# A softplus in a state-space kernel: the last sum moved to TensorE, two absolute values and relus to an eviction, and one product a chunk from GpSimd to VectorE

## The chip, the cores and the metric

The kernel runs on one core of one Trainium2 chip. A core has five engines with a queue each, worked off in order: TensorE (PE, with its weight loads PEld), VectorE (DVE), ScalarE (ACT), GpSimd (POOL) and SyncE (SP, which here only issues DMAs). The metric is device time in microseconds; the median of several runs is compared.

## What is computed

Two layers over one image of 64 x 64 positions (L = 4096) with 96 channels. Layer 0 is a two-dimensional selective scan and isn't touched. Layer 1 is a Mamba block with 192 inner channels and 16 states. Cut to what matters here:

```python
delta = jax.nn.softplus(jnp.einsum('blr,dr->bld', dt, W_dt) + b_dt)
dA = jnp.exp(delta[..., None] * A)
dBu = delta[..., None] * Bm[:, :, None, :] * xc[..., None]
def step(h, inp):
    dA_t, dBu_t, C_t = inp
    h = dA_t * h + dBu_t
    y = jnp.einsum('bdn,bn->bd', h, C_t)
    return (h, y)
```

`delta` is called dt in the kernel, `xc` is u, and delta times xc is w. The kernel computes softplus(x) as max(x, 0) plus S(|x|), where S is a product of two factors made from sigmoids and squares of |x|: acc, the first sigmoid, times (a square of q, plus SOFT_D).

## The kernel before

**Units.** Layer 1 is cut into four chunks of 1024 positions (CH). The 192 channels times 16 states of a chunk are done in 24 units of 128 rows, so 96 units s in all; a unit has step i = s mod 24 within its chunk. Three units in a row share the same two states: their B and C rows are the same, and they hold 64 channels each, once for either state. For each unit: dA = exp(A dt) on ScalarE (`decay`), f = B times w, the scan h over 1024 positions on VectorE (`scan`), h times C on GpSimd (`times_c`), and a sum over states into y on TensorE (`fold`, three units later).

**Who makes f.** The first unit of each group of three (s divisible by 3, `on_pool`) gets its f from GpSimd: B is loaded by DMA onto 128 rows (`load`), multiplied by w in place (`pool_f`, two units ahead), and dA is put into the PSUM tile f0. For the other two, TensorE spreads B over the rows into the PSUM tile f1 (`spread`), and VectorE multiplies it by w, into f0 or back into f1. So a VectorE instruction of the steady state has one operand in PSUM.

**Order.** The order on each engine is written out by hand: the class `Ordered` (L384, with the issuing call in L400, which is why nearly all instructions bear that line) chains each engine's instructions in the order of the calls in `run` (L2040). In each step s it calls: the next piece of `between` (L1944: the next chunk's projections, the last parts of its softplus, the former chunk's output), fillers on TensorE (`hold`), `spread` if s is divisible by 3, the loads, the decays of units s+1 or s+2, the next piece of `soft` (L2011), the unit's f and scan, then whatever `between` left as `late` on ScalarE, then `times_c` of unit s-1 and `pool_f` of unit s+2 on GpSimd, then the fold of unit s-3. `hold` (L1654) adds matmuls with zeros into an open y: they do nothing but keep TensorE busy.

**The next chunk's front.** While chunk c is scanned, chunk c+1 is prepared. `front_v` (L1518) makes dt's argument in three parts of 512 columns in the one PSUM bank `misc`, and ScalarE copies each to SBUF. `soft` then runs through the steps i, counted from at = 3 in chunk 0 and from 0 elsewhere: Abs of the whole dt to q at at+7; the two sigmoids (`soft_logistic`, L225) at at+9, for which ScalarE loads a table and then loads that of Exp again; the first Square at at+11. B of the next chunk, fetched as `flat`, is split into three bfloat16 parts by four small GpSimd instructions at at+10 (`split_b`, L1481: cast, subtract, cast, subtract), stored at at+13 and loaded at at+18; TensorE needs those parts for `spread`. `soft_parts` (L1987) does the rest in three steps (i = 16 to 18 in chunk 0, 13 to 15 in chunks 1 and 2): the second Square from q into PSUM on ScalarE (sq), then on VectorE `soft_times` (L245: (sq + SOFT_D) times acc) and max(dt, 0) plus that. At at+16 and at+17 GpSimd makes w = dt times u (`front_w`); dt and w are then copied by DMA onto the rows of the units (`front_dup`).

The last chunk has no next one, so `soft` and `soft_parts` do nothing in it.

Of the kernel before, what the change touches and what calls it, by code (L numbers as in the profile page):

```python
# [13 lines left out]
AF = mybir.ActivationFunctionType  # L14
ALU = mybir.AluOpType
# [10 lines left out]
P = 128  # L26
HALF = DI - P
GRP = 3
NB = 512
NCH = L // NB  # L30
CH = 1024
NSC = L // CH
# [5 lines left out]
UNIT = len(UNITS[0]) + len(UNITS[1])  # L38

PAIRS, GROUPS = NS // 2, DI // HALF  # L40
LAG = 3
WIDE = P
DUPS = {15: ((0, "dt"),), 16: ((1, "dt"),), 17: ((0, "w"),), 18: ((1, "w"), (2, "dt")), 19: ((2, "w"),)}

# [15 lines left out]
SOFT_ROOT = SOFT_K**0.5  # L60
# [164 lines left out]
def soft_logistic(nc, k, e, last, q):  # L225

    for to, i in ((last, 0), (q, 1)):
        nc.scalar.activation(to, e, AF.Sigmoid, scale=-1.0, bias=k["soft"][:, i : i + 1])


def soft_square(nc, k, q, i):

    nc.scalar.activation(
        q, q, AF.Square, scale=(1.0, SOFT_ROOT)[i], bias=k["soft"][:, 2 + i : 3 + i]
    )
# [9 lines left out]
def soft_times(nc, last, q, out):  # L245

    nc.vector.scalar_tensor_tensor(out, q, SOFT_D, last, ALU.add, ALU.mult)
# [1058 lines left out]
class Layer1:  # L1306
# [171 lines left out]
            flat, self.bc_dram[0, c].rearrange("n (j k) -> (n j) k", k=NS * CH // P)  # L1478
        )

    def split_b(self, c):  # L1481

        nc, b = self.nc, self.chunks[c]["flat"]
        self.at = c
        self.chunks[c]["split"] = parts = self.tile("flat", [P, 3, NS * CH // P], "split", BF16)
        nc.gpsimd.tensor_copy(parts[:, 0, :], b)
        nc.gpsimd.tensor_sub(b, b, parts[:, 0, :])
        nc.gpsimd.tensor_copy(parts[:, 1, :], b)
        nc.gpsimd.tensor_sub(parts[:, 2, :], b, parts[:, 1, :])

    def store_b(self, c, queue=None):
        (queue or self.nc.sync).dma_start(
# [25 lines left out]
    def front_v(self, c, q):  # L1518
        nc, of = self.nc, self.chunks[c]
        if "dt" not in of:  # L1520
            self.at = c
            of["dt"] = self.tile("dt", [P, CW], "dt")
            of["acc"], of["q"] = self.tile("sp", [P, CW], "acc"), self.tile("sp", [P, CW], "q")
        ps = self.misc(c, [P, NB], f"pv{q}")
        yield from self.steps(
            self.product(ps, q, self.dt_taps(of["dbl"])),
            lambda: nc.scalar.copy(of["dt"][:, self.part(q)], ps),
        )

    def front_w(self, c, col, engine):  # L1530
        of = self.chunks[c]
# [28 lines left out]
        return self.chunks[c]["dup"][i % GROUPS][name]  # L1560

    def on_pool(self, s):
        return s % GROUPS == 0 and 0 < s < NSC * UNIT

    def load(self, part, s):

        if s >= NSC * UNIT:
            return
        name, (c, i) = "BC"[part], divmod(s, UNIT)
        self.at = s  # L1570
        self.units[s][name] = to = self.tile(name, [P, CH], name)
        for share, state in enumerate(UNITS[1][i // GROUPS]):
            row = self.bc_dram[part, c, state : state + 1, :]
            self.nc.sync.dma_start(to[self.half1(share), :], row.to_broadcast([HALF, CH]))
# [25 lines left out]
    def scan(self, s):  # L1600
        self.at, of = s, self.units[s]
        c, i = divmod(s, UNIT)
        if not self.on_pool(s):
            if i % GROUPS == (1 if s > GROUPS else 0):
                self.f = self.tile("f", [P, CH], "f0")
            of["f"] = self.b if i % GROUPS == 2 else self.f
            self.nc.vector.tensor_mul(of["f"], self.b, self.of_unit("w", s))
        of["h"] = self.tile("h", [P, CH + SHIFT], "h")
        self.nc.vector.tensor_tensor_scan(
            of["h"][:, SHIFT:], of["dA"], of["f"], self.last[:, i : i + 1] if c else 0.0,  # L1610
            ALU.mult, ALU.add,
        )
# [41 lines left out]
    def hold(self, s, ahead):  # L1654

        c, i = divmod(s, UNIT)
        at = i - (3 if c == 0 else 0)
        if c == NSC - 1 and i:
            n = 0 if 7 <= i <= 12 else 1 if not ahead else 2 if i % GROUPS == 0 else 0
        else:  # L1660
            n = ({0: 1, 9: 1, 12: 1, 15: 1} if ahead else {-2: 2, -1: 1, 1: 2, 12: 1, 13: 2, 14: 2, 15: 2}).get(at, 0)
        open_y = [(k, g) for k, g in ((c, 2), (c, 0), (c - 1, 2)) if self.is_open(s - ahead, k, g)]
        for _ in range(n if open_y else 0):
            k, g = open_y[0]
            self.nc.tensor.matmul(
                self.chunks[k][f"y{g}"], self.k["zero"], free(self.k["within"], (1, NB)),
                start=False, stop=False,
            )
# [130 lines left out]
    def start(self):  # L1799
# [17 lines left out]
        dbl = of["dbl"] = self.tile("dbl", [ROWS, CH], "dbl")  # L1817
        acc, sq = of["acc"], of["q"] = [self.tile("sp", [P, CW], n) for n in ("acc", "q")]
        dt = of["dt"] = self.tile("dt", [P, CW], "dt")
# [32 lines left out]
            do(self.product(pv[p], p, self.dt_taps(dbl)))  # L1852
        self.flat_b(0)
        self.load(1, 0)
        self.split_b(0)
        self.store_b(0, nc.gpsimd)

        next_u = self.chunks[1]
# [128 lines left out]
    def soft_parts(self, c):  # L1987

        of = self.chunks[c]
        for p in range(3):  # L1990
            col = self.part(p)
            ps = self.misc(c, [P, NB], f"sq{p}")
            self.late = lambda: self.nc.scalar.activation(
                ps, of["q"][:, col], AF.Square, scale=SOFT_ROOT, bias=self.k["soft"][:, 3:4]
            )
            yield
            soft_times(self.nc, of["acc"][:, col], ps, ps)
            self.nc.vector.scalar_tensor_tensor(
                of["dt"][:, col], of["dt"][:, col], 0.0, ps, ALU.max, ALU.add
            )  # L2000

    def all_between(self):
        for c in range(NSC):
# [7 lines left out]
    def soft(self, c):  # L2011

        at = 3 if c == 0 else 0
        for i in range(UNIT):
            if c + 1 < NSC:
                nc, k = self.nc, self.k
                dt, acc, q = (self.chunks[c + 1].get(n) for n in ("dt", "acc", "q"))
                if i == at + 7:
                    nc.scalar.activation(q, dt, AF.Abs)
                elif i == at + 9:  # L2020
                    soft_logistic(nc, k, q, acc, q)
                elif i == at + 11:
                    soft_square(nc, k, q, 0)
                elif i == at + 6:
                    self.flat_b(c + 1)
                elif i == at + 10:
                    self.split_b(c + 1)
                elif i == at + 13:
                    self.store_b(c + 1)
                elif i == at + 18:  # L2030
                    self.load_b(c + 1)
                elif i == at + 16:
                    self.front_w(c + 1, slice(0, CH), nc.gpsimd)
                elif i == at + 17:
                    self.front_w(c + 1, slice(CH, CW), nc.gpsimd)
                for g, name in DUPS.get(i - at, ()):
                    self.front_dup(c + 1, g, names=(name,))
            yield

    def run(self):  # L2040
# [5 lines left out]
        for s in range(n):  # L2046
# [30 lines left out]
            if self.on_pool(s + 2):  # L2077
                self.pool_f(s + 2)
            if s >= LAG:
                if s < n - 1:  # L2080
# [191 lines left out]
```

## Time and profile before

| | us |
|---|---|
| median of 3 runs | 521.02 (519.98 to 521.06) |
| the profiled execution | 520.83 |
| its span in the profile | 519.0 |
| first scan of chunk 0, 1, 2, 3 (start) | 182.24, 262.38, 344.37, 427.70 |
| last scan ends | 507.6 |

| steady rows of layer 1 | count | mean ns |
|---|---|---|
| GpSimd h<-h,C, 128x1024 | 95 | 2395 |
| GpSimd B<-B,w, 128x1024 | 31 | 2373 |
| VectorE scan h<-dA,last,f, 128x1024 | 47 | 2347 |
| VectorE f<-f,w, 128x1024 | 65 | 1221 |
| ScalarE dA<-dt,A, 128x1024 | 65 | 1140 |
| ScalarE table load | 24 | 1283 |
| TensorE y<-within,zeros (the fillers), 128x512 | 134 | 652 |

A row of the profile names the line, engine, operation, output <- inputs by the program's tile names, their shapes, the count, and the time. In a timeline a row has the start and the duration, and in brackets how long the engine stood idle before it and what released it. Rows of one engine overlap by up to 0.1 us, so what a repeated instruction costs is read from one start to the next. Times are from the start of the span.

### The profile page before, as it was taken

What the parts mean: (1) busy time and instruction counts of PE and PEld (TensorE: products, weight loads), DVE (VectorE), ACT (ScalarE), POOL (GpSimd) and SP (SyncE); (2) the same over time, 40 slices, a digit from 0 to 9 for tenths busy, and PEclk for the clock granted to TensorE, in tenths of its full rate; (3) what the DMA queues carried; (4) which work ended last, traced back from release to release, by engine and by line L of the source; (5) the groups of instructions that cost most, each with busy time, mean ns of one, the idle gap of its engine ahead of it and who ended that gap; (6) DMA issues with size and microseconds to landing.
All of it is one profiled execution on the core that took longest, in us unless ns stands there. A gap on an engine that the chain in (4) does not pass through costs nothing. (4 is left out here: it accounts for less than half of the span.)

```text
span 519.0 us, 5048 instructions
## 1 busy us (share of the span) xinstructions
PE 454.0 (87%) x1487; PEld 171.6 (33%) x1487; DVE 450.5 (87%) x458; ACT 310.4 (60%) x475; POOL 368.3 (71%) x249
## 2 busy tenths in 40 slices
PE   4999999989879999887768988879689979987994
PEld 3445446546533323222112322212112322222323
DVE  6896999946661899989999999989999999999993
ACT  4637996378735896893395883475783366253220
POOL 8034010017620669999999999998999999999980
PEclk9997999999999999999799989979968989998898
DMA  6100930000000584435993446973536993454301
GB/s 180 30 5 12 257 129 0 0 1 1 2 31 5 144 206 126 132 82 133 234 215 97 124 126 153 232 186 80 132 82 140 235 237 82 122 136 97 81 0 38
DMA packets 28536, 55.90 MB, mean 108 GB/s; under 512 B 13186, under 2 KB 14974, under 8 KB 28244
## 3 DMA queue, kind: packets, MB, share of 16 engines
q1 hardware_dynamic: 26596, 53.58, 42.4%
q10 hardware_dynamic: 1808, 1.72, 1.1%
q8 instruction: 13, 0.21, 0.2%
q0 software_dynamic: 96, 0.20, 0.2%
q14 instruction: 23, 0.19, 0.1%
HBM read 41.86 MB, written 2.65 MB: 86 GB/s over the span
## 5 line engine op out<-in xcount | busy, mean ns | idle before, releaser
L400 POOL TENSOR_TENSOR h<-h,C 128x1024 f32<-128x1024 f32 x96 | 226.7, 2383 | 11.4 <-DVE h L400 6.8
L400 DVE TENSOR_TENSOR_SCAN h<-dA,last,f 128x1024 f32<-128x1024 f32 (+1 forms) x48 | 111.6, 2325 | 4.6
L400 PE MATMUL y<-h,both 128*64 128x512 f32 x382 | 113.4, 673 | 1.0 <-POOL h L400 1.0
L400 ACT ACTIVATE f<-dt,A 128x1024 f32<-128x1024 f32 x31 | 34.7, 1118 | 89.9 <-DVE h L400 89.8
L400 DVE TENSOR_TENSOR f<-f,w 128x1024 f32<-128x1024 f32 x65 | 79.3, 1221 | 4.7 <-PE f L400 2.4
L400 POOL TENSOR_TENSOR B<-B,w 128x1024 f32<-128x1024 f32 x31 | 73.5, 2373 | 2.0 <-DMA B<-bc_dram 2.0
L400 ACT ACTIVATE dA<-dt,A 128x1024 f32<-128x1024 f32 x65 | 73.6, 1140 | 1.7 <-DMA dt<-dt 1.7
L400 PE MATMUL y<-within,zeros 128*128 128x512 f32 x134 | 72.0, 652 | 0.0
L400 DVE TENSOR_TENSOR_SCAN h<-f,last,B 128x1024 f32<-128x1024 f32 x24 | 55.9, 2328 | 0.0
L400 PE MATMUL pc<-pad,cw 96*128 96x464 f32 (+1 forms) x144 | 54.9, 540 | 0.5 <-ACT v L400 0.5
L400 PEld LDWEIGHTS y<-h,both 128*64 128x64 f32 x382 | 23.3, 146 | 65.9 <-issue 43.6
L400 DVE TENSOR_TENSOR_SCAN h<-dA,f 128x1024 f32<-128x1024 f32 x17 | 38.9, 2287 | 1.5
L400 PEld LDWEIGHTS y<-within,zeros 128*128 128x128 f32 x134 | 23.0, 196 | 49.5 <-issue 49.5
L400 PE MATMUL f<-parts,pick 48*128 48x512 bf16 x62 | 20.7, 418 | 20.3 <-DVE h L400 20.3
L400 PEld LDWEIGHTS pc<-pad,cw 96*128 96x128 f32 x144 | 28.3, 199 | 27.0 <-issue 22.4
L400 ACT ACT_TABLE_LOAD x24 | 30.8, 1283 | 2.1 <-PEq L2262 1.7
L400 POOL TENSOR_SCALAR ln_small<-ln_small 128x4 f32<-128x4 f32 x8 | 1.9, 236 | 37.4 <-DVE ln_small L400 35.7
L400 POOL MEMSET wda<- 128x4 f32 (+3 forms) x8 | 1.0, 120 | 31.1 <-ACT wda L400 31.1
L400 PE MATMUL pc<-xn,cw 96*64 96x512 f32 (+1 forms) x60 | 21.5, 601 | 0.7 <-ACT xn L400 0.7
L400 PE MATMUL po<-v,w_o 128*128 128x256 f32 (+1 forms) x48 | 15.5, 458 | 3.0 <-DVE x L400 2.3
L400 PE MATMUL po<-sz,w_out 128*128 128x512 f32 x36 | 18.0, 610 | 0.0
L400 PEld LDWEIGHTS <-pick 48*128 48x128 bf16 x62 | 4.0, 96 | 41.1 <-DVE h L400 22.7
(236 smaller groups left out, 713.9 us busy)
## 6 DMA issues: line engine op xcount, KB each, us to landing
C<-bc_dram SPq DMA_DIRECT2D x64, 256.0 KB, 5.0
B<-bc_dram SPq DMA_DIRECT2D x62, 256.0 KB, 4.0
dt<-dt SPq DMA_DIRECT2D x12, 256.0 KB, 4.5
w<-q SPq DMA_DIRECT2D x12, 256.0 KB, 5.8
dt<-dt SPq DMA_DIRECT2D x18, 128.0 KB, 6.0
w<-q SPq DMA_DIRECT2D x18, 128.0 KB, 4.7
wB<-rows_dram SPq DMA_DIRECT2D x1, 1472.0 KB
wC<-rows_dram SPq DMA_DIRECT2D x1, 1472.0 KB
```

The source lines that it names most:

```text
L400: ins = it(*args, **kw)
```

## The change

- dt's eviction becomes two ScalarE instructions: relu into dt, absolute value into q. The single Abs at at+7 goes.
- The sigmoids come a step earlier (at+8); both Squares run over all 1536 columns from SBUF to SBUF (at+11, at+12).
- In each of the three steps of `soft_parts`, VectorE makes acc = (q + SOFT_D) times acc with all operands in SBUF; TensorE adds dt and acc in `misc` by two matmuls with the identity; ScalarE copies the sum to dt.
- `split_b` becomes two halves: cast on ScalarE and subtraction on GpSimd at at+9, the same again at at+11. In the start of the layer GpSimd still does all.
- Unit 18 of each chunk but the last (OFF_POOL) gets its f from VectorE: no B load and no GpSimd product, dA in SBUF, and unit 17's f goes to f0 so that f1 is free for the spread of unit 18.
- The fillers at at+13 to at+15 go: seven matmuls a chunk.

```diff
+OFF_POOL = 18
...
-    def split_b(self, c):
+    def split_first(self, c, cast=None):
 
         nc, b = self.nc, self.chunks[c]["flat"]
         self.at = c
         self.chunks[c]["split"] = parts = self.tile("flat", [P, 3, NS * CH // P], "split", BF16)
-        nc.gpsimd.tensor_copy(parts[:, 0, :], b)
+        (cast or nc.scalar.copy)(parts[:, 0, :], b)
         nc.gpsimd.tensor_sub(b, b, parts[:, 0, :])
-        nc.gpsimd.tensor_copy(parts[:, 1, :], b)
-        nc.gpsimd.tensor_sub(parts[:, 2, :], b, parts[:, 1, :])
+
+    def split_rest(self, c, cast=None):
+
+        b, parts = self.chunks[c]["flat"], self.chunks[c]["split"]
+        (cast or self.nc.scalar.copy)(parts[:, 1, :], b)
+        self.nc.gpsimd.tensor_sub(parts[:, 2, :], b, parts[:, 1, :])
...
-        ps = self.misc(c, [P, NB], f"pv{q}")
-        yield from self.steps(
-            self.product(ps, q, self.dt_taps(of["dbl"])),
-            lambda: nc.scalar.copy(of["dt"][:, self.part(q)], ps),
-        )
+        ps, col = self.misc(c, [P, NB], f"pv{q}"), self.part(q)
+
+        def evict():
+            nc.scalar.activation(of["dt"][:, col], ps, AF.Relu)
+            nc.scalar.activation(of["q"][:, col], ps, AF.Abs)
+
+        yield from self.steps(self.product(ps, q, self.dt_taps(of["dbl"])), evict)
...
     def on_pool(self, s):
-        return s % GROUPS == 0 and 0 < s < NSC * UNIT
+        c, i = divmod(s, UNIT)
+        return s % GROUPS == 0 and 0 < s < NSC * UNIT and (i != OFF_POOL or c == NSC - 1)
...
-        if s >= NSC * UNIT:
+        if s >= NSC * UNIT or part == 0 and not self.on_pool(s):
...
-            if i % GROUPS == (1 if s > GROUPS else 0):
+            if i % GROUPS == 0 or i % GROUPS == 1 and self.on_pool(s - 1):
                 self.f = self.tile("f", [P, CH], "f0")
-            of["f"] = self.b if i % GROUPS == 2 else self.f
+            of["f"] = self.b if i % GROUPS == 2 and self.on_pool(s + 1) else self.f
...
-            n = ({0: 1, 9: 1, 12: 1, 15: 1} if ahead else {-2: 2, -1: 1, 1: 2, 12: 1, 13: 2, 14: 2, 15: 2}).get(at, 0)
+            n = ({0: 1, 9: 1, 12: 1} if ahead else {-2: 2, -1: 1, 1: 2, 12: 1}).get(at, 0)
...
-            ps = self.misc(c, [P, NB], f"sq{p}")
-            self.late = lambda: self.nc.scalar.activation(
-                ps, of["q"][:, col], AF.Square, scale=SOFT_ROOT, bias=self.k["soft"][:, 3:4]
-            )
+            dt, acc = of["dt"][:, col], of["acc"][:, col]
+            soft_times(self.nc, acc, of["q"][:, col], acc)
+            ps = self.misc(c, [P, NB], f"sum{p}")
+            for i, term in enumerate((dt, acc)):
+                self.nc.tensor.matmul(ps, self.k["ident"], term, start=i == 0, stop=i == 1)
+            self.late = lambda: self.nc.scalar.copy(dt, ps)
             yield
-            soft_times(self.nc, of["acc"][:, col], ps, ps)
-            self.nc.vector.scalar_tensor_tensor(
-                of["dt"][:, col], of["dt"][:, col], 0.0, ps, ALU.max, ALU.add
-            )
...
-                if i == at + 7:
-                    nc.scalar.activation(q, dt, AF.Abs)
+                if i == at + 8:
+                    soft_logistic(nc, k, q, acc, q)
                 elif i == at + 9:
-                    soft_logistic(nc, k, q, acc, q)
+                    self.split_first(c + 1)
                 elif i == at + 11:
                     soft_square(nc, k, q, 0)
+                    self.split_rest(c + 1)
+                elif i == at + 12:
+                    soft_square(nc, k, q, 1)
                 elif i == at + 6:
                     self.flat_b(c + 1)
-                elif i == at + 10:
-                    self.split_b(c + 1)
```

More of the change, by code (lines that the diff above doesn't have):

```diff
@@ L1854, in start @@
         self.load(1, 0)
-        self.split_b(0)
+        self.split_first(0, nc.gpsimd.tensor_copy)
+        self.split_rest(0, nc.gpsimd.tensor_copy)
         self.store_b(0, nc.gpsimd)
@@ L2016, in soft @@
                 nc, k = self.nc, self.k
-                dt, acc, q = (self.chunks[c + 1].get(n) for n in ("dt", "acc", "q"))
-                if i == at + 7:
-                    nc.scalar.activation(q, dt, AF.Abs)
+                acc, q = (self.chunks[c + 1].get(n) for n in ("acc", "q"))
+                if i == at + 8:
+                    soft_logistic(nc, k, q, acc, q)
                 elif i == at + 9:
-                    soft_logistic(nc, k, q, acc, q)
+                    self.split_first(c + 1)
                 elif i == at + 11:
                     soft_square(nc, k, q, 0)
+                    self.split_rest(c + 1)
+                elif i == at + 12:
+                    soft_square(nc, k, q, 1)
                 elif i == at + 6:
                     self.flat_b(c + 1)
-                elif i == at + 10:
-                    self.split_b(c + 1)
                 elif i == at + 13:
```

## The prediction

> **What bounds the kernel now.** I read the busy shares first, then the VectorE timeline from 180 us on, then GpSimd's and ScalarE's beside it, and last the few places where VectorE and GpSimd both read SBUF.
>
> ```profile
> PE 454.0 (87%) x1487; PEld 171.6 (33%) x1487; DVE 450.5 (87%) x458; ACT 310.4 (60%) x475; POOL 368.3 (71%) x249
> ```
>
> The shares average two layers, so they don't decide. The VectorE timeline of chunk 0 does (start, duration; idle in brackets):
>
> ```profile
> 227.09 2.29 DVE L400 TENSOR_TENSOR_SCAN h<-dA,f 128x1024 f32<-128x1024 f32 x1
> 230.51 2.29 DVE L400 TENSOR_TENSOR_SCAN h<-f,B 128x1024 f32<-128x1024 f32 x1 [1.14 <-POOL B L400]
> ...
> 236.45 0.67 DVE L400 SCALAR_TENSOR_TENSOR sq<-sq,acc 128x512 f32<-128x512 f32 x1
> 237.16 0.69 DVE L400 SCALAR_TENSOR_TENSOR dt<-dt,sq 128x512 f32<-128x512 f32 x1
> 237.76 1.23 DVE L400 TENSOR_TENSOR f<-f,w 128x1024 f32<-128x1024 f32 x1
> ```
>
> From the first scan (182.24) to the last (507.6) VectorE stands still four times: 1.14 us here, 1.45 at 346.7, 0.43 and 0.49 in the last chunk. VectorE is the bound of layer 1; what is taken from it or put on it counts in full. GpSimd runs beside it almost without a gap:
>
> ```profile
> 219.48 4.73 POOL L400 TENSOR_TENSOR h<-h,C 128x1024 f32<-128x1024 f32 x2
> 224.17 0.28 POOL L400 CAST split<-flat 128x128 bf16<-128x128 f32 x1
> ...
> 225.78 2.40 POOL L400 TENSOR_TENSOR h<-h,C 128x1024 f32<-128x1024 f32 x1
> 228.11 2.37 POOL L400 TENSOR_TENSOR B<-B,w 128x1024 f32<-128x1024 f32 x1
> ```
>
> It starts a product every 2.335 us (7.0 for three), and its B<-B,w feeds a scan: ended at 230.48, scan of unit 15 started at 230.51. A group of three units costs VectorE 9.43 to 9.61 us and GpSimd 4 x 2.335 = 9.34. GpSimd has no slack for a long wait. ScalarE has idle time, but in bursts; this is the burst that matters:
>
> ```profile
> 216.47 1.12 ACT L400 ACTIVATE f<-dt,A 128x1024 f32<-128x1024 f32 x1
> 217.53 1.13 ACT L400 ACTIVATE dA<-dt,A 128x1024 f32<-128x1024 f32 x1
> ...
> 221.29 1.28 ACT L400 ACT_TABLE_LOAD   x1
> 222.59 1.58 ACT L400 ACTIVATE acc<-q,soft 128x1536 f32<-128x1536 f32 x1
> 224.19 1.58 ACT L400 ACTIVATE q<-q,soft 128x1536 f32<-128x1536 f32 x1
> ...
> 225.96 1.28 ACT L400 ACT_TABLE_LOAD   x1
> 227.26 1.12 ACT L400 ACTIVATE f<-dt,A 128x1024 f32<-128x1024 f32 x1
> ```
>
> **Part by part.** All of it happens three times, for chunks 1 to 3 while chunks 0 to 2 are scanned; the fourth chunk's steps stay.
>
> VectorE, removed: three pairs of 512 columns, each 236.45 to 237.76 = 1.31 us: -3.93 a chunk. Added: three single acc products, about 0.62 each by the same rows: +1.86. Added: unit 18's f. A unit with f on VectorE takes 3.57 us (two from 276.00 to 283.16), one with GpSimd's product 2.42 (283.16 to 285.59): +1.15. Sum -0.9 a chunk, -2.7 in all.
>
> GpSimd: a B product (2.335) and two casts (0.36 each) go, 3.1 a chunk. As VectorE is the bound this is worth at most the 1.14 us above. SP's queue loses two loads a chunk: nothing, since GpSimd waited for a B load only once (2.03 us before 189.07), and that load stays.
>
> ScalarE: Abs over 1536 (1.48) becomes three of 512 at eviction (nearest rows: a copy from PSUM 0.58, an Identity 0.69), three squares of 512 (0.68) become one of 1536 (1.56), three evictions (0.58) and two casts are new: 2 to 3 us more. From 200 to 290 us ScalarE is busy 59.73 of 90, so the amount costs nothing; its order does.
>
> **The hand-over of the split.** The first subtraction on GpSimd now waits for a cast on ScalarE, and behind it on GpSimd's queue stand the h products and the next B product that a scan needs. The order of the built program puts the cast behind: decay, decay, table load, two sigmoids, u's eviction, table load, decay. Chunk 0: the two decays end 218.58; table and sigmoids 4.39 (221.29 to 225.68) to 222.97; u 0.58, last 0.08, table 1.30, decay 1.05: 225.98. The cast on ScalarE has no row: between a 128x1 copy (0.18) and a 128x384 copy (0.46); I take GpSimd's own 0.28. Cast done 226.3. GpSimd is at that place at 221.8, where h of unit 10 ends. So it stands 4.5 us. Then 0.43 for the subtraction and 7.0 for h, h, B: 233.8. Unit 15's scan starts there and not at 230.51: +3.3, with the old 1.14 inside.
> Chunk 1, the same chain from 289.31 (decays to 291.40, +4.39, +0.58, +0.09, +1.30, +1.05, +0.28): cast 299.1, where GpSimd is free at 292.8; B product out at 306.6, and the scan of that chunk's unit 12 was at 302.37: +4.25. Chunk 2 from 372.65 has no u: cast 381.85, B at 389.35 for 385.71: +3.65. Sum +11.2. The decay behind the sigmoids is in time (298.8 for a scan at 300.1); the last Square too (ends near 306.4 without any wait, acc then comes after 308.8).
>
> **The acc product reads q and acc, both in SBUF**, where sq was in PSUM; in steady state no VectorE operation of this kernel has two SBUF inputs. The start of the layer has some, VectorE first:
>
> ```profile
> 172.28 0.69 DVE L400 SCALAR_TENSOR_TENSOR acc<-q,acc 128x512 f32<-128x512 f32 x1
> 178.33 1.09 DVE L400 SCALAR_TENSOR_TENSOR acc<-q,acc 128x512 f32<-128x512 f32 x1
> ```
> ```profile
> 177.85 1.04 POOL L400 COPY dt<-dt 64x512 f32<-64x512 f32 x1
> 178.83 1.07 POOL L400 COPY w<-q 64x512 f32<-64x512 f32 x1
> ```
>
> The second took 0.40 longer: it seems to begin when GpSimd's copy ends, and GpSimd's next copy took 1.07 where others take 0.62. The Trainium skill, "SBUF — State Buffer", section "Who interferes with whom", speaks against this edit: a VectorE instruction with two SBUF inputs and a GpSimd one that reads SBUF exclude each other, and the later waits until the earlier is over. By the uncontended row acc costs 0.62; by the rule, up to one whole product more (0 to 2.34 each, 0 to 21 us for nine). The copies are short, so the rows alone can't choose; I take the rule and work out the phase. Let the late B product end at 0: scan to 2.26; GpSimd does the second subtraction (0.43) and h to 2.77: acc waits 0.5. GpSimd goes on about 0.55 late: h to 5.65, h to 8.0; the next acc comes at 6.95 and waits 1.05; the third comes at 12.2 with h running until 13.3: 1.1. Together 2.6 a chunk, the same in each, because the same product starts the clock: +7.8.
>
> **TensorE.** Six matmuls against ident for seven fillers a chunk, both 128x512 (the fillers take 0.65, started every 0.43 to 0.5): nothing. In chunks 1 and 2 the third sum is in step 15, its spread is needed one scan later: hidden, with about 1 us to spare. In chunk 0 the third sum stands in step 18 directly ahead of spread(18), and unit 18's f, now on VectorE, needs that at once: after acc one matmul (0.5, by the fillers), the spread (0.60, the row at 241.37), two hand-overs of some 0.05: +1.2, once; bounds 0.6 (if spread overlaps) and 2 (if TensorE comes cold: the two fillers at 345.06 took 2.08). dt's copy out of PSUM comes later than the vector addition did, but w and the copies of dt wait on steps far behind: nothing, up to 1 if the covering group were gone.
>
> **Sum:** 11.2 + 7.8 - 2.7 + 1.2 = +17.5 us. The profiled execution took 520.83 (span 519.0, 1.8 around it), 0.2 under the median; so 521.0 + 17.5 = 538.5, and a span of 536.5.
>
> **Rivals.**
> GpSimd is not held, and the trade is worth its face. If the cast were there when GpSimd comes (before 221.8, 292.8 and 376.1, so 4.5 to 6.4 us earlier than worked out), GpSimd, 3.1 us lighter, would run ahead and wait for each scan; acc would start with the scan's end and be first. -2.7 - 1.1 + 1.2 gives 518.4. For it: GpSimd already waits 0.2 to 0.7 for scans in chunks 1 and 2. Against: the table load can't move ahead of the decays, which wait for scans. 7%.
> Held, but no exclusion: 521.0 + 9.7 = 530.7. For it: only short copies show the exclusion. 17%.
> Exclusion, but a hand-over mostly hidden: about 521.0 + 5 = 526. 7%.
> A harder exclusion, each acc waiting nearly a whole product, or GpSimd's next one going first: 8 to 13 us more, 547 to 552. 9%.
> As worked out, 534 to 543: 58%. 2% for no change.
>
> **How the numbers follow.** The likeliest case gives 538.5. The range reaches to the case without exclusion and to the upper side of the likeliest: 529 to 543. A measurement here tells 0.2% (1 us) from no change: faster 0.07, within 0.02, slower 0.91.
>
> **What would show it.** Right: in the profile after, GpSimd's small flat subtraction has 4 to 6.5 us idle before it, released by ScalarE; VectorE's scans of unit 15 (chunk 0) and 12 (chunks 1 and 2) wait 3.7 to 4.5 for B; acc<-q,acc lasts 1.2 to 1.8 instead of 0.69, and the h product after it 0.5 longer; in chunk 0 one f waits about 1.2 for TensorE. Wrong: acc at 0.69 takes off 7.8; no idle ahead of the subtraction takes off 11.2; a long wait for q or for dt would be something that I put at nothing.

## The result, and the profile after

| | before | after |
|---|---|---|
| median, us | 521.04 (519.98 to 522.67, 4 runs) | 553.35 (549.0 to 555.77, 4 runs) |
| ratio to before | | 1.0608, 95% interval 1.0534 to 1.0682 |
| profiled execution; its span | 520.83; 519.0 | 549.0; 547.1 |
| first scan of chunk 0, 1, 2, 3 to the first of the next chunk (chunk 3: to the start of its last scan) | 80.14, 81.99, 83.33, 78.63 | 86.91, 94.13, 92.65, 77.91 |

Slower by 32 us, where 17.5 was predicted. A ratio leaves out executions far above the fastest of their kernel (four of six in e1, four of 22 in e14), so it needn't be that of the two medians. The profiled execution is the fastest of the four after; the account below is of it, 28 us above the profiled one of before.

The busy shares of after, to be held against the first line of the prediction:

```profile
PE 456.4 (83%) x1481; PEld 171.9 (31%) x1481; DVE 464.0 (85%) x452; ACT 315.5 (58%) x490; POOL 362.1 (66%) x240
```

VectorE has six instructions less and is busy 13.5 us longer: some instruction of it has become slow. Every chunk with a next one is longer, by 6.8, 12.1 and 9.3 us; the last, which the change hardly touches, is not. The VectorE timeline of after in chunk 0 (start, duration, what, and in brackets the idle time ahead of it):

```profile
224.46 1.23 DVE L401 TENSOR_TENSOR f<-f,w 128x1024 f32<-128x1024 f32 x1 [0.90 <-PE f L401]
...
236.22 2.29 DVE L401 TENSOR_TENSOR_SCAN h<-f,B 128x1024 f32<-128x1024 f32 x1 [4.62 <-POOL B L401]
238.43 1.02 DVE L401 SCALAR_TENSOR_TENSOR acc<-q,acc 128x512 f32<-128x512 f32 x1
...
250.38 1.23 DVE L401 TENSOR_TENSOR f<-f,w 128x1024 f32<-128x1024 f32 x1 [1.75 <-PE f L401]
```

The scan waits 4.62 us for GpSimd's B, and unit 18's f 1.75 for TensorE: both were foretold (4.44 and 1.2). The wait of the f at 224.46 was not. GpSimd's timeline there:

```profile
228.79 0.43 POOL L401 TENSOR_TENSOR flat<-flat,split 128x128 f32<-128x128 f32 x1 [6.17 <-ACT split L401]
229.18 4.69 POOL L401 TENSOR_TENSOR h<-h,C 128x1024 f32<-128x1024 f32 x2
233.84 2.35 POOL L401 TENSOR_TENSOR B<-B,w 128x1024 f32<-128x1024 f32 x1
```

That is the hand-over as worked out: the subtraction stands 6.17 us for ScalarE's cast (7.2 and 6.0 in chunks 1 and 2), then come h, h and the B that the scan needs. What was not foretold is in chunk 1 (all engines; rows of several engines and PE's weight loads left out):

```profile
315.70 2.35 DVE L401 TENSOR_TENSOR_SCAN h<-f,last,B 128x1024 f32<-128x1024 f32 x1 [4.56 <-POOL B L401]
315.94 7.03 POOL L401 TENSOR_TENSOR h<-h,C 128x1024 f32<-128x1024 f32 x3
...
317.97 7.85 DVE L401 SCALAR_TENSOR_TENSOR acc<-q,acc 128x512 f32<-128x512 f32 x1
...
322.84 2.43 POOL L401 TENSOR_TENSOR B<-B,w 128x1024 f32<-128x1024 f32 x1
...
329.49 2.68 POOL L401 TENSOR_TENSOR h<-h,C 128x1024 f32<-128x1024 f32 x1 [4.22 <-DVE h L401]
```

One product of 512 columns, 0.67 us by itself, takes 7.85. It starts behind its scan at 317.97 and ends at 325.82, 0.55 after GpSimd's B product ended at 325.27: it lasted through the rest of one h product, two more, and the B product. GpSimd ran dry only because the scan that releases its next h stands behind this very product. Chunk 2 shows the same (7.88); in chunk 0 the three took 1.02, 1.75 and 0.67, and the first two of these got in when GpSimd's running product ended, although its next one was ready. The second and third of chunks 1 and 2 took 0.67, since GpSimd was waiting then.

How the stretch from the first scan to the start of chunk 3's last sums up, by the table of stretches (us, then busy time of each engine), before and after:

```profile
sum 324.09, PE 283.03 PEld 81.90 DVE 311.94 ACT 189.05 POOL 310.28; mean PE 70.76 PEld 20.48 DVE 77.98 ACT 47.26 POOL 77.57
```
```profile
sum 351.60, PE 285.38 PEld 82.09 DVE 325.94 ACT 194.05 POOL 304.09; mean PE 71.35 PEld 20.52 DVE 81.49 ACT 48.51 POOL 76.02
```

27.5 us longer: VectorE is busy 14.0 us more and idle 13.5 more. GpSimd's 6.2 less are worth nothing.

| term of the sum | predicted | in the profile after |
|---|---|---|
| hand-over: VectorE's waits for B | +11.2 | 4.62 + 4.56 + 3.79, less the old 1.14: +11.8 |
| acc's waits for GpSimd | +7.8 | nine acc, 21.8 us, less 9 x 0.67: +15.8 |
| the trade on VectorE | -2.7 | busy +14.0 less those 15.8: -1.8 |
| f waiting for TensorE | +1.2 | 0.90 + 1.75 + 0.60 + 0.35, less the old 1.45 + 0.43 + 0.49: +1.2 |
| sum | +17.5 | +27.0 |

The 0.5 us that the sum lacks are gaps too short to be listed.

### The profile page after: what moved, and what is told of

Its sections match the earlier page's. It is cut to its first block, busy times and chain, and to the rows that moved or that the text cites. A ratio compares the mean times of both kernels' runs of the same rounds, so it can differ in the third digit from the quotient of the medians.

```text
span 547.1 us, 5030 instructions
## 1 busy us (share of the span) xinstructions
PE 456.4 (83%) x1481; PEld 171.9 (31%) x1481; DVE 464.0 (85%) x452; ACT 315.5 (58%) x490; POOL 362.1 (66%) x240
## 5 line engine op out<-in xcount | busy, mean ns | idle before, releaser
L401 DVE TENSOR_TENSOR_SCAN h<-dA,last,f 128x1024 f32<-128x1024 f32 (+1 forms) x50 | 116.3, 2326 | 5.1
L401 DVE TENSOR_TENSOR f<-f,w 128x1024 f32<-128x1024 f32 x68 | 83.1, 1222 | 6.0 <-PE f L401 3.6
L401 ACT ACTIVATE dA<-dt,A 128x1024 f32<-128x1024 f32 x68 | 77.1, 1141 | 12.2 <-DVE h L401 11.2
L401 POOL TENSOR_TENSOR B<-B,w 128x1024 f32<-128x1024 f32 x28 | 66.4, 2372 | 1.5 <-DMA B<-bc_dram 1.5
L401 DVE TENSOR_TENSOR_SCAN h<-f,last,B 128x1024 f32<-128x1024 f32 x22 | 51.3, 2331 | 8.3 <-POOL B L401 8.3
L401 PE MATMUL y<-within,zeros 128*128 128x512 f32 x92 | 50.1, 652 | 0.0
L401 PE MATMUL sum<-acc,ident 128*128 128x512 f32 x18 | 11.7, 738 | 19.0 <-DVE acc L401 19.0
L401 ACT COPY dt<-sum 128x512 f32<-128x512 f32 x9 | 5.3, 586 | 36.2 <-PE sum L401 36.2
L401 PEld LDWEIGHTS y<-within,zeros 128*128 128x128 f32 x92 | 15.3, 194 | 33.3 <-issue 33.3
L401 DVE SCALAR_TENSOR_TENSOR acc<-q,acc 128x512 f32<-128x512 f32 x12 | 24.5, 2045 | 0.0
```

Source lines behind the costliest of these rows:

```text
L401: ins = it(*args, **kw)
```

## The experiments

Two theories at first. Mine: the hand-over's place costs its 11 us whatever else happens, and acc costs more than worked out because GpSimd instructions whose inputs are ready go first. The rival: acc is late for another reason (its Square, the order on VectorE), and the second SBUF operand is a bystander. "Port" stands below for whatever keeps a VectorE product with two SBUF operands and a GpSimd product from running at once. For reference, the kernel before took 520.98 beside e1 to e4, 522.13 beside e5 to e7, 521.58 beside e8 to e11, 520.96 beside e13 and e14, and 520.94 beside e18.

**e1, the changed kernel once more.**

> The changed kernel once more, unaltered, to see how much the long acc differs from one execution to the next. Queue theory (GpSimd keeps the read port for as long as its next instruction is ready, and whether acc gets in between two of them is decided by a few hundredths of a microsecond): the times spread over 549 to 556 us and the first acc of at least one chunk has another length than 1.02, 7.85 and 7.88. Data theory (acc waits for one GpSimd instruction at most, and the 7.85 comes from an operand that is late in chunks 1 and 2): the same lengths in the same chunks. Both: the idle time ahead of the flat subtraction is 6.2, 7.2 and 6.0 again.

555.11 (545.66 to 555.67), ratio 1.0524 (1.047 to 1.0578), where the medians alone give 1.066. The profiled execution is one of 555.54. The waits for B were 4.65, 4.56 and 3.82; acc took 7.87 and 7.95 in chunks 1 and 2, and in chunk 0, on the timeline:

```profile
236.38 7.05 POOL L401 TENSOR_TENSOR h<-h,C 128x1024 f32<-128x1024 f32 x3
238.29 5.69 DVE L401 SCALAR_TENSOR_TENSOR acc<-q,acc 128x512 f32<-128x512 f32 x1
```

The same place that took 1.02 us in the first profile takes 5.69 here, again until GpSimd's third h had ended. So this is an outcome that can fall either way. The nine acc took 25.5 us, not 21.8, and VectorE waited 5.9 us for f, not 3.6: together 6.0 of the 6.5 us between the two profiled executions. The idle time ahead of the flat subtraction, put at 6.2, 7.2 and 6.0 again by both theories, was 8.55 in chunk 1, with the same wait for B.

**e2, acc with one SBUF operand.** The second Square goes to PSUM, part by part, as before.

```diff
-            soft_times(self.nc, acc, of["q"][:, col], acc)
+            soft_times(self.nc, acc, of["sq"], acc)
```

> The changed kernel with the second Square put into PSUM in three parts as before, so that acc has one SBUF input; the sum on TensorE and the hand-over of the split stay. Queue theory: every acc takes 0.67, VectorE wins back the 15.8 us that they are over 0.62 each in the profile after (549.0), less about 0.5 because TensorE can't start a sum early: 533 to 535, with the waits of 4.6, 4.6 and 3.8 for B unchanged. Data theory: the first acc of chunks 1 and 2 stays long, over 545.

538.88 (535.67 to 539.91), ratio 1.0326 (1.0287 to 1.0365). The acc row:

```profile
L401 DVE SCALAR_TENSOR_TENSOR acc<-sq,acc 128x512 f32<-128x512 f32 x9 | 6.1, 675 | 0.9 <-ACT sq L401 0.9
```

All nine take 0.66 to 0.69. The waits for B stay (13.1 us). So the second SBUF operand holds some 14 us. The time missed the 533 to 535 expected: VectorE's waits for f grew from 3.6 to 7.2 us.

**e3, the casts back on GpSimd at at+10, all else as changed.**

> The changed kernel with the two casts back on GpSimd at at+10, so that GpSimd waits for nothing there; acc stays in SBUF. Hand-over theory: the waits of the scans for B (4.62, 4.56, 3.79) fall to at most 1.2 together, about 11.8 us less by themselves; GpSimd then has another phase when acc comes, so the accs can take from 0.67 to 8 each: 535 to 545 against 553. If the waits for B came from GpSimd's load and not from the cast, they stay and the time is 550 or more.

535.04 (534.25 to 536.38), ratio 1.0281 (1.0248 to 1.0314). No scan waits for B any more. The first acc of each chunk still stands (3.41, 1.68 and 6.40 us), and VectorE now comes earlier and waits for the Square as well:

```profile
DVE acc L401 <- ACT q L401: 3.7, 3, 1.7
```

**e4, both undone.**

> Both undone: acc reads its square from PSUM and GpSimd casts for itself; the relu and Abs at eviction, the sum on TensorE and unit 18's f on VectorE stay. If port and hand-over are the whole loss, what is left is the trade at face value: 3 x (-2.07 + 1.15) = -2.8 on VectorE, +1.8 to 2.3 for f of unit 18 in chunk 0 behind the third sum, up to -1.1 for the old wait for B: 519 to 521. If there is a third cause, over 523.

528.3 (525.29 to 530.37), ratio 1.0145 (1.011 to 1.018). This missed what I expected by 7 us: a third cost had been covered by the first two. VectorE's waits in it (total, times, longest):

```profile
DVE f L401 <- PE f L401: 8.0, 8, 2.6
DVE acc L401 <- ACT sq L401: 2.5, 3, 1.1
```

Before, the same stretch had none for a Square, and for f:

```profile
DVE f L400 <- PE f L400: 2.4, 3, 1.4
```

**e5, the hand-over at a better place.** e2, with ScalarE's casts at at+9 and at+12 and GpSimd's subtractions two steps behind them; the store moves to at+15 (diff against e2).

```diff
                 elif i == at + 11:
...
+                    self.minus_first(c + 1)
...
+                elif i == at + 14:
+                    self.minus_rest(c + 1)
```

> As the run with the Square in PSUM, with the split still shared by ScalarE and GpSimd, but GpSimd's two subtractions stand later in its queue (at+11 and at+14, store at at+15), where ScalarE's casts have long been done. The work is the same, only the place differs. Hand-over theory: no idle ahead of the subtractions, no wait of a scan for B over 0.5: 518 to 521. If the cost of the hand-over were that of the handing itself (a semaphore between two engines), 530 or more.

529.73 (528.73 to 531.3), ratio 1.0155 (1.0108 to 1.0202); no wait for B. That is e4's time, which has no hand-over at all: handing work over costs nothing measurable there; standing for it at the head of GpSimd's queue does. The 518 to 521 expected were missed by 9 us, as in e4 by the third cost (waits of 8.1 us for f and 4.7 for a Square).

**e6, the hand-over alone, in the kernel before** (with the sigmoids at at+8).

> The kernel before with the split's hand-over alone: sigmoids at at+8, casts on ScalarE, subtractions on GpSimd at at+9 and at+11; nothing else changed. Hand-over theory: scans wait about 4.6, 4.6 and 3.8 for B, 12 us less the old 1.1: 531 to 533. If the hold only comes about together with the other edits: 521 to 523.

533.59 (531.39 to 536.03), ratio 1.0205 (1.0151 to 1.0259): +11.5, against +11.2 worked out.

```profile
DVE h L400 <- POOL B L400: 12.9, 3, 4.6
```

**e7, the second SBUF operand alone, in the kernel before.** The second Square, one of 1536 columns at at+12, writes SBUF, and the nine products read it there.

```diff
-            soft_times(self.nc, of["acc"][:, col], ps, ps)
+            soft_times(self.nc, of["acc"][:, col], of["q"][:, col], ps)
```

> The kernel before with the port's edit alone: the second Square stays in SBUF over all 1536 columns, and the nine products with acc read both factors from SBUF and write to PSUM as before. One-instruction theory (the prediction's): each waits 0 to 2.3 us for GpSimd, so 9 x 1.2 = 10 at a middling phase and 21 at most: 525 to 542. Queue theory: single products wait for more than one GpSimd instruction, up to where GpSimd's next one needs a scan that stands behind the product: some last 3 to 10 us, the time is 530 to 560. No port at all: 521.

541.77 (541.54 to 541.93), ratio 1.0375 (1.033 to 1.042): +19.6. The nine products together:

```profile
L400 DVE SCALAR_TENSOR_TENSOR sq<-q,acc 128x512 f32<-128x512 f32 x9 | 25.2, 2796 | 0.0
```

At 0.67 each they would be 6.0; the other 19.2 are the loss. The first of each chunk took 6.13, 4.89 and 5.50, the second 0.67, the third 2.2. The total alone fits both theories (525 to 542 and 530 to 560); these lengths, over 0.67 + 2.34, fit only the one without the bound of one instruction. The operand alone, with nothing else of the change, does it: the rival falls.

**e8 to e11: the third cost.** Each is e4 with one thing set back: the seven fillers (e8), the sigmoids at at+9 (e9), unit 18's f on GpSimd (e10). e11 sets all three back; in it each acc comes a step behind its Square, and part of dt is copied onto the units' rows before its sum is in, so that some rows have the relu alone.

> The kernel with both causes undone (split's products in PSUM, casts on GpSimd), and the seven filler products at steps 13 to 15 of a chunk restored, nothing else. What is left open by that kernel's 528.3 us are some 5 us that neither cause holds, and its VectorE shows short waits for TensorE's f (0.35 and 0.54 a chunk, 1.60 and 0.66 beside the accumulation). If those come of a TensorE that has cooled without its fillers, the waits of 0.35 and 0.54 go and the time falls to 525 to 526. If they come of the places of the products and sigmoids, the fillers change nothing or cost something: 528 to 529.

> Both causes undone, and the sigmoids back at step 9 from step 8. The theory for the third cause: u's eviction stands behind the earlier sigmoids on ScalarE and so holds its PSUM bank, and the next products of TensorE and an f behind them are late (1.60 and 0.66 us in the profile of both undone). Then those two waits go, and the time is 525.5 to 527. Against it: if the sigmoids' place doesn't matter, 528 to 529; the Squares then come later too, and the accumulation may wait for them longer than the 0.80, 0.63 and 1.07 it waits now (up to 1 us more each), which would take the gain back.

> Both causes undone, and unit 18's second f back on GpSimd in every chunk, so that this part of the change is undone as well. By the sum of the prediction VectorE then has 1.15 us less in each of three chunks, and the wait of 2.61 us of that f for TensorE in chunk 0 is gone: 528.3 less 3.45 less 2.6 = 522.2. Against it: GpSimd gets 2.2 us more in each of those chunks, and if its order with the scans was already tight there (it had no slack of its own left in the later steps), the scans wait for B by up to as much and the time stays at 526 to 529.

> The part that gives, alone: relu and absolute value at dt's eviction and the sum on TensorE, with the Squares into PSUM and dt copied out by ScalarE at the end of its step; fillers, sigmoids at step 9, unit 18's f on GpSimd and the casts on GpSimd all as in the kernel before. If the trade on VectorE is worth what the prediction put on it (two operations on the scans' engine removed and one left in each of nine places, 2.07 us a chunk, three chunks), 521.0 less 6.2 = 514.8, and 515 to 518 with some waits of the accumulation for its Square. If GpSimd is the bound in these chunks once VectorE is shorter (it has about as much to do as VectorE), the time stays at 519 to 521. Over 523 would say that the sum on TensorE itself costs what it saves.

| kernel | median, us | ratio to before |
|---|---|---|
| e4 | 528.3 | 1.0145 (1.011 to 1.018) |
| e8 | 537.09 (534.39 to 540.76) | 1.0317 (1.0284 to 1.035) |
| e9 | 530.77 (528.72 to 536.61) | 1.0217 (1.0176 to 1.0258) |
| e10 | 521.23 (518.48 to 524.59) | 0.9998 (0.9976 to 1.002) |
| e11 | 530.33 (529.61 to 533.76) | 1.0201 (1.0169 to 1.0232) |

The missing fillers (seven calls a chunk, 42 rows in all in the profile) are not what e4 lacks: with them back, VectorE's wait for f grows from 8.0 to 14.5 us, so leaving them out is worth 9 us in a kernel with the sum.

```profile
DVE f L401 <- PE f L401: 14.5, 8, 4.0
```

The sigmoids seem better early (e9's interval just meets e4's): back at at+9, VectorE waits 6.5 us for the Squares, not 2.5. e11, where I had put 515 to 518, has fillers and late sigmoids and waits 10.8 us for f and 7.7 for Squares, where e10 waits 6.8 and 3.9. Unit 18's f on VectorE is what e4 loses by: 7 us, as e10's expectation had it (522.2). But e10 shows more than I had asked of it: its page has VectorE busy 5.4 us less than before, at the same time.

```profile
PE 454.0 (87%) x1481; PEld 171.4 (33%) x1481; DVE 445.1 (85%) x449; ACT 316.3 (61%) x490; POOL 368.4 (71%) x249
```

GpSimd's 368.4 us are the 368.3 of before.

**e13 and e14: without the sum** (e13 against e4, e14 against e10; dt then stays the relu alone).

```diff
-            ps = self.misc(c, [P, NB], f"sum{p}")
-            for i, term in enumerate((dt, acc)):
-                self.nc.tensor.matmul(ps, self.k["ident"], term, start=i == 0, stop=i == 1)
...
-                self.nc.scalar.copy(dt, ps)
```

> Both causes undone, and the sum left out: the identity products of TensorE and ScalarE's copies of the sum into dt are gone, so dt stays the relu alone; all else as it was. If the 7 us by which both undone lies over what its parts should give come of the sum on TensorE (its queue stands for acc for 8.6 us, takes some 1.9 a part, and VectorE's f waits 8.0 for it), the time falls to 518 to 520: VectorE's waits for f go back to about 2.4, and what is left is the trade on VectorE of 2.7 us under the kernel before. If they come of unit 18's f on VectorE, which waits for its place in TensorE's queue whatever the sum does, the time stays at 524 to 528.

> The same without the sum, and unit 18's f on GpSimd: what the shorter VectorE is worth at most. VectorE has 6.2 us less to do than in the kernel before (2.07 a chunk, three chunks), in a stretch in which it was busy for 312 of 324 us and GpSimd for 310. If VectorE's time is the bound there, 515 to 516. If GpSimd's is, which has as much to do as before, the time stays at 519 to 521, and the shortening was worth nothing without the shift of unit 18's f.

e13: 522.45 (521.34 to 528.45), ratio 1.0047 (1.002 to 1.0074). e14: 521.14 (517.13 to 526.45), ratio 0.9987 (0.9964 to 1.0011). So the third cost is a pair: with unit 18's f on VectorE the sum costs 5.9 us (e4 less e13), with that f on GpSimd it costs nothing (e10 less e14). From e4 to e13 the waits for f fall from 8.0 to 3.6 us and those for Squares from 2.5 to 0.9. The longest of them, 2.61 us, was unit 18's f in chunk 0, whose spread stands behind the third sum on TensorE's queue, which stands for acc; in e13 it does not wait. That this order also makes the other waits was not tried apart. And a shorter VectorE is worth nothing measurable: e14 has removed most and is no faster than before.

**e12, e15, e16, e17: the port by itself.** Each is the kernel before with a test behind its last write; only the test's rows count. Blocks of GpSimd products of 128x1024 are queued, and VectorE does one product of 512 columns in the midst.

> The kernel before, with a test added behind its last write, so its total time says nothing. In each block GpSimd does one product of 128 by 1024, ScalarE copies 512 columns of it (some 0.6 us and the hand-over, say 0.8 in all), GpSimd has meanwhile n more products of 2.4 us queued with nothing to wait for, and VectorE does one scalar_tensor_tensor of 512 columns that needs ScalarE's copy, so that it arrives while the first of the n runs. Then GpSimd waits for it. n is 0, 1, 2, 3, 4, 6; once with both of VectorE's inputs in SBUF, once a plain product with both in SBUF, once with one of them in PSUM. Last come two blocks (2 and 4 products) in which each further GpSimd product is released by ScalarE only after the one ahead of it ended. If GpSimd keeps the port for as long as its next instruction is ready, VectorE's instruction takes 0.67 and n times 2.4 less 0.8: 0.67, 2.3, 4.7, 7.0, 9.4 and 14.2 for both forms, 0.67 from PSUM for all n, and about 2.3 in the last two blocks. If it waits for one product at most, as the prediction had it, 2.3 for every n from 1 to 6.

Every product with both operands in SBUF took 1.71 us, however many GpSimd products were queued, and every one with an operand in PSUM 0.69 (in a row: count, min/median/max in ns, first and last start):

```profile
L400 DVE SCALAR_TENSOR_TENSOR acc_port<-q_port x8: 692/1714/1717, 515.1 to 691.0; 128x512 f32<-128x512 f32 x8
L400 DVE TENSOR_TENSOR acc_port<-q_port x6: 692/1714/1716, 571.4 to 612.1; 128x512 f32<-128x512 f32 x6
L400 DVE SCALAR_TENSOR_TENSOR acc_port<-sq_port,q_port x6: 692/692/692, 627.8 to 666.8; 128x512 f32<-128x512 f32 x6
```

(The 692 of the first two rows are the blocks without a queued product.) The theory that GpSimd keeps the port as long as its next product is ready failed here. But the queued products wrote one tile, with 0.08 us between any two, which the kernel's do not have.

> The test behind the kernel before once more, now with each of GpSimd's queued products in a tile of its own: when they wrote one tile, each waited for the end of the one ahead, 0.08 us stood between any two, and VectorE's product always got in after the first (1.71 us for every n). n is 0, 1, 2, 3, 4, 6 with ScalarE's copy at 512 columns; then n is 4 with the copy at 32 to 480 columns in steps of 64, so that VectorE's product arrives at eight different times within the first of the four; then one plain product from SBUF and one with a factor in PSUM. If the port goes on to GpSimd's next product as long as that one is ready without a gap, the times grow with n by about 1.9 (0.7, 1.7, 3.6, 5.5, 7.4, 11.2), stand at 7 to 8 for every arrival at n of 4, and at 0.7 from PSUM. If one product is the most that it waits for, all are 1.7 to 2.3, and the 7.9 us of the changed kernel had another cause. If it is a race between the two at each boundary, the eight arrivals scatter over 2, 4, 6 and 8.

With a tile each, and no gap:

```profile
L400 DVE SCALAR_TENSOR_TENSOR acc_port<-q_port x14: 692/2258/2582, 519.4 to 675.6; 128x512 f32<-128x512 f32 x14
```

2.2 to 2.6 for one to six queued products and for eight arrivals: let in at the first end.

> The test behind the kernel before a third time: four queued GpSimd products of 128 by 1024, each in its own tile, and VectorE's product with both factors in SBUF. In 17 blocks VectorE's product now stands directly behind a scan on VectorE, as it does in the kernel, and the scan is 768 to 1024 columns long in steps of 16, so that the product is reached between some 0.6 us before the end of the first queued GpSimd product and about its end. In 17 more blocks ScalarE releases it after two copies, the second of 512 to 1024 columns in steps of 32, over about the same times. In the tests so far it arrived 0.6 us or more ahead of that end and always got in there (1.7 to 2.6 us). If what counts is the arrival in the last half microsecond, blocks of both kinds that arrive there stand for one or more products longer (about 3 to 8 us) and the others 1 to 1.3. If it is the place directly behind a scan, the 17 blocks with a scan show 7 to 8 us whatever the arrival, and those behind ScalarE do not. If neither, all get in at the first end, at 0.7 to 1.3 us, and the cause of the 7.9 us in the kernel stays open.

```profile
L400 DVE SCALAR_TENSOR_TENSOR acc_port<-q_port x17: 2757/2758/2783, 522.4 to 763.2; 128x512 f32<-128x512 f32 x17
L400 DVE SCALAR_TENSOR_TENSOR acc_port<-dA_port,q_port x17: 693/835/2900, 776.0 to 989.7; 128x512 f32<-128x512 f32 x17
```

Neither the place behind a scan nor the moment shuts it out for more than one further product. The scans of this test had both factors in SBUF and waited for the port themselves (3.88 us for 768 columns), so those 17 products arrived elsewhere than planned. The 2.90 arrived 0.05 us before an end and got in at the next.

> The test behind the kernel before a fourth time, now with the kernel's own order. In each of 25 blocks GpSimd first has k products of 2.3 us with nothing to wait for (k from 1 to 5), VectorE meanwhile does four scans with one factor in PSUM, as the kernel's, and directly behind the fourth the product with both factors in SBUF; GpSimd's further four products are each released by one of the scans. So k says how far GpSimd lags, and how many of its products wait with their release already given when VectorE's product arrives: none at k of 1, one or two at 3, three at 4, all at 5. The last scan has 1024, 928, 832, 736 and 640 columns, which moves the arrival by 0.2 us a step. If a lagging GpSimd with releases already given is what shuts VectorE out, the products take 7 to 9 us at k of 4 and 5, 3 to 5 at 3, and 0.7 to 2.4 at 1 and 2. If the port changes hands at every end, as in the tests so far, none takes over 2.9, and the 7.9 us of the kernel stays without a cause.

```profile
L400 DVE SCALAR_TENSOR_TENSOR acc_port<-acc_port,q_port x25: 912/1536/3901, 527.5 to 968.0; 128x512 f32<-128x512 f32 x25
```

With the kernel's own order, 23 of 25 got in at the first end, two at the second (3.70 and 3.90, both at k of 1, where I had expected none). In the four tests that is 82 of 85 at the first end, and none beyond the second.

**e18, the question put to the changed kernel itself:** acc and its sum behind the step's f and not ahead of it.

```diff
+        if self.mid:
+            self.mid()
         self.nc.vector.tensor_tensor_scan(
```

> The changed kernel with one thing moved: each of the products with two SBUF factors, and the sum behind it, comes behind its step's f on VectorE instead of ahead of it, so that it is reached some 1.3 us later and not directly behind a scan; GpSimd's order is as it was. The tests of the port by itself have let VectorE in at the first end of a GpSimd instruction in 82 of 85 blocks, at the second in three, never later; in the changed kernel the first product of chunks 1 and 2 stood behind four. If what shuts it out there is a fixed state of GpSimd's queue (four released instructions on end), the product takes 7.9 less 1.3, about 6.5 us, in those chunks, and the time stays within some 3 us of 553. If it is the moment of the arrival, one of the three first products at least gets in at the first end (0.7 to 2.4 us), and each that does takes about 5 us off: 540 to 548.

557.78 (556.22 to 558.81), ratio 1.07 (1.0666 to 1.0733). On the timeline of chunk 1:

```profile
326.50 6.55 DVE L401 SCALAR_TENSOR_TENSOR acc<-q,acc 128x512 f32<-128x512 f32 x1
330.11 2.39 POOL L401 TENSOR_TENSOR B<-B,w 128x1024 f32<-128x1024 f32 x1
```

The first acc of chunks 0 to 2 took 4.32, 6.55 and 6.61: 1.3 us later in, and out again 0.55 us after GpSimd had run dry. So a later arrival did not free these three. But standing until GpSimd runs dry is no rule either. The third acc of chunk 0 in this very run got in at the first end, and GpSimd's next product, ready behind it, took 2.81 us:

```profile
256.23 1.41 DVE L401 SCALAR_TENSOR_TENSOR acc<-q,acc 128x512 f32<-128x512 f32 x1
257.05 2.81 POOL L401 TENSOR_TENSOR q<-dt,u 128x1024 f32<-128x1024 f32 x1
```

So did the first two of chunk 0 in the first profile (1.02 and 1.75), the first of chunk 1 in e3 (1.68) and the third of each chunk in e7 (2.2). Both outcomes occur while all engines work, and what decides between them is open. The tests by themselves lacked the DMAs and the work of ScalarE and TensorE, and no run here has tried those apart.

## Why the prediction was wrong

The direction was right, and so were the hand-over and that acc and GpSimd's products exclude each other; three of the four terms hold within 1 us. **The failed step** is the size of acc's wait: "by the rule, up to one whole product more (0 to 2.34 each, 0 to 21 us for nine)". The bound of one product is false in this kernel: 7.85 less 0.67 is 7.2 us, three times that. The term of 7.8 us measured 15.8 in the profile, and 8.0 of the 10 us that the sum lacked lie there; the hand-over lacked 0.6 and the trade 0.9.

The step took its bound from the Trainium skill ("SBUF — State Buffer", section "Who interferes with whom"), by which the shared port pair is an exclusive lock. That whoever issues first has it for the whole instruction is said there of VectorE's two-port modes, and I carried it over to two SBUF inputs. The tests of the port by itself agree (82 of 85). The page doesn't say whose turn is next when both stand ready, and I read it as VectorE's. The prediction gave 9% to "GpSimd's next one going first: 8 to 13 us more, 547 to 552", which is what happened in chunks 1 and 2; the range of 529 to 543 left it out. Its working of the phase fits the first two acc of chunk 0 (waits of 0.35 and 1.08 us for 0.5 and 1.05) and fails elsewhere: it had the same in each chunk, but the later two of chunks 1 and 2 took 0.67, because the first had already let GpSimd run dry. What makes GpSimd go first in one place and VectorE in another stays open.

**The hand-over** was right in place, chain and size: 4.62, 4.56 and 3.79 us of wait, where 4.44, 4.25 and 3.65 come out of the working; e6 alone gives +11.5. GpSimd itself stood longer ahead of the subtraction than put, 6.17, 7.2 and 6.0 us for 4.5, 6.3 and 5.75. The cast without a row took 0.28, as put.

**TensorE.** Unit 18's f waited 1.75 for the 1.2 worked out, within its bounds. That the whole term is +1.2 is luck: three more f's wait for TensorE, 0.90 in chunk 0 and 0.60 and 0.35 in chunk 1, and three waits of before are gone (2.37 us). The exchange of fillers for identity products was put at nothing as well; that holds only while the other losses cover it, for without them the sum costs 5.9 us beside unit 18's f (e4 less e13). In chunk 0 u's eviction stands behind the earlier sigmoids (it starts at 225.33, behind a table load and 3.1 us of sigmoids). That this is what holds TensorE there was not tried apart: e9 moves the sigmoids back and its f waits sum to much the same (7.4 for 8.0).

**The trade on VectorE** came out as busy time (-1.8 for -2.7), but the rule behind it, "what is taken from it or put on it counts in full", holds one way only. What was put on VectorE did count. What is taken is worth nothing: e10 and e14 have 5.4 and 6.8 us less on VectorE and stand within 0.2% of before. In the four chunks of before VectorE was busy for 311.9 us and GpSimd for 310.3; with one shortened the other may hold, and I had credited GpSimd's load with nothing. That GpSimd is what holds e14 isn't shown: its VectorE also waits 6.6 us for f. And in e13 both have less to do than before, VectorE 2.2 us and GpSimd 5.7, at no gain; what takes it back was not tried apart. So even without both losses the change had nothing to win: e4 is 1.45% slower than before.

## What to carry to other kernels

Before giving a VectorE instruction a second SBUF operand, look at what GpSimd has queued at that moment, not at the one instruction that is running: here the first product of a chunk, 0.67 us long, stood for up to 7.95. When work is handed from one in-order engine to another, work out when the giver gets to it and place the taker's half behind that (e5 did, e2 did not, and they lie 9 us apart). Where two engines are nearly equally busy, don't count work removed from one in full: here 5.4 and 6.8 us less gave nothing measurable.

## What was not expected of the hardware

- VectorE with both operands in SBUF stood through up to four GpSimd instructions with their inputs ready (7.85, 7.88, 7.87, 7.95 us), but through one only in 82 of 85 blocks when nothing else of the kernel ran; in the kernel, too, some got in at the first end (1.02, 1.75, 1.68, 1.41, 2.2).
- The first GpSimd product behind one of VectorE's takes longer by what it waits: 2.8 us for 2.33.
- A GpSimd product of 128x1024 whose two inputs are one tile took 1.89 us, with two tiles 2.33 to 2.40.
- A scan of 768 columns with both factors in SBUF took 3.88 us beside GpSimd; one of 736 columns with a factor in PSUM took 1.66.
- The changed kernel's executions spread over 545.7 to 555.8 us, those of the kernel before over 518.2 to 524.6.
